# Graph attention over sorted edges: softmax batches of 24 groups in place of 32, and one joint tile with one 128-column product per 128 edges

## The chip, the cores and the metric

The kernel runs on one core of one Trainium2 chip. The metric is the time that the device takes for one execution, in microseconds (us). The kernel before takes 5138.95 us, the median of 3 runs (5133.07 to 5140.92).

A core has engines that run side by side, each through its own list of instructions: TensorE (PE in the profile; PEld are its weight loads), VectorE (DVE), ScalarE (ACT), GpSimd (POOL) and SyncE (SP). They wait for each other by semaphores. Transfers between DRAM and on-chip memory are DMAs: an engine issues them, and they run apart from it.

## The reference: what is computed

One layer of a graph network with attention: 12,500 nodes with 64 features each (`x`), and 400,000 directed edges with 64 features each (`edge`), sorted by their destination `dst`.

```python
h_src, h_dst = nfeats[src], nfeats[dst]
e = leaky_relu(concat([h_src, h_dst, efeats]) @ W_attn + b_attn, 0.01)[:, 0]
m = concat([h_src, efeats]) @ W_ne
ex = exp(e - segment_max(e, dst)[dst])
alpha = ex / segment_sum(ex, dst)[dst]
z = segment_sum(alpha[:, None] * m, dst)
out = layernorm(x + relu(concat([nfeats, z]) @ W_out))
```

Each edge gets a score, the scores are normalised by a softmax over the edges of one destination, and the edges' messages are summed with these weights. `W_ne` is linear, so the kernel sums the raw features (the source's row and the edge's features) with the weights alpha, and multiplies by `W_ne` and `W_out` once per node at the end.

## The kernel before

**Tiling.** The edges are cut into 782 groups of 512 (128 partitions x 4 edges). Four groups make a part, and up to 32 groups (`BG`) a softmax batch. The list `sizes` (L345 to L353) is [30], 23 times 32, then 12 and 4: 26 batches, 196 parts; a full batch has 8 parts.

**A part, up to its scores.** `gather` (L134 to L153) takes two tiles: `ze` for the edge features and `zx` for the rows of the sources. SyncE issues one DMA for the part's edge features (L140): 512 KB, where each partition gets 1024 adjacent bytes per group. GpSimd issues 16 indirect DMAs (L149), each of which fetches 128 rows, one per partition. In later batches the row comes from a DRAM table, whose rows hold the 64 features and, in column 64, the source's part of the score. The first batch ("plain") starts before that table is there: it fetches from `x` itself and works out the score in L169 to L171. `scores` (L155 to L185) is VectorE's: multiply the edge features by their weights (L165), reduce (L167), add the source's score (L172), build `hot`, a 0/1 matrix that says which of 48 neighbouring nodes (`S`) an edge goes to (L174), add the destination's score (L179 to L183; it comes as a row `wrow` by a SyncE DMA, L159, and is spread over the partitions by TensorE, L161), leaky ReLU (L184). The scores go into the batch's tile `y`.

**A batch.** When all parts of a batch are scored, `softmax` (L224 to L319) normalises the whole batch at once. It transposes `y` (L252), runs scans along the sorted destinations, with small TensorE products between them to carry values across rows (L190, L198), and leaves `alpha` (L307). It takes from the batch before the carried maximum and sum (`carry`), and it needs the destinations of the neighbouring edges, `d3`, which `neighbours` (L203) loads by four SyncE DMAs (L218). A batch smaller than `BG` clears `d3` and `y` first (L208 and in the main loop).

**A part, after its softmax.** `aggregate` (L321 to L342): VectorE makes the weights `w` = `hot` x `alpha` (L324). TensorE multiplies: for each of 4 groups and 4 edges per partition, one product with `ze` as its weights and one with `zx` (L332), 64 columns each, written to the lower and the upper 64 partitions of `pg`; `w` with its 48 columns moves through. That is 32 products per part; each appears in the trace as two weight loads and two matmuls (float32). VectorE then adds `pg` to `acc`, which holds the sums of all nodes on chip (L342).

```python
pg = psum.tile([P, SG, P], F32, name="pg")[:, :, 0:S]
for g in range(n):
    for t in range(T):
        for at, z in ((0, ze), (D, zx)):
            nc.tensor.matmul(pg[at:at + D, g, :], z[:, g, t, 0:D], w[:, g, t, :],
                             start=(t == 0), stop=(t == T - 1))
```

**Buffers.** `ze` and `zx` have 11 buffers each (`ZB`), so that 11 parts can be on chip between their gathers and their products; `hot` has 9 (`HB`), `w` and `pg` have 2, `d3` and `y` 2, `alpha` 1. A gather into a tile has to wait until the products of the part that had the tile are over.

**What sets the order.** All loops are unrolled when the program is built. The framework puts each engine's instructions in order by a planner with estimated costs, and adds the semaphores; on the chip each engine keeps its order. SyncE's list has the edge features, `wrow`, `d3` and the index loads; GpSimd's has the indirect gathers and little else; ScalarE's has copies, exponentials and DMAs for other work. Five parts of the first batch are gathered ahead of the main loop (L369, L415).

**Around the loop.** In the first 300 us or so the kernel also prepares the table. In batches from the third on, `own_part` (L432; L446, L450) does one piece of x @ W_out after each part's sums, until all nodes are done. `finish_sorted` (L491) multiplies `acc` by the joint weights (L538), adds, normalises and stores.

Of the kernel before, what the change touches and what calls it, by code (L numbers as in the profile page):

```python
# [9 lines left out]
F32 = mybir.dt.float32  # L10
I32 = mybir.dt.int32
AF = mybir.ActivationFunctionType
OP = mybir.AluOpType
AX = mybir.AxisListType

P = 128
T = 4
GE = P * T
# [7 lines left out]
S = 48  # L26
BG = 32
SG = 4
HQ = 4
EW = 65  # L30
ZB = 11
HB = 9
NBC = 4
# [5 lines left out]
def sorted_path(ctx, tc, x, dst, idx, edge, w_ne, w_attn, b_attn, w_out, out, flag):  # L39
# [6 lines left out]
    nc = tc.nc  # L46
    N, D = x.shape
# [6 lines left out]
    RP = REST // T  # L54
# [36 lines left out]
    feats = loop.enter_context(tc.tile_pool(name="feats", bufs=ZB))  # L91
# [41 lines left out]

    def gather(g0, n, srcs, b0, plain):  # L134

        ze = feats.tile([P, SG, T, D], F32, name="ze")
        zx = feats.tile([P, SG, T, EW], F32, name="zx")
        whole = min(n, NG - 1 - g0)
        if whole:
            nc.sync.dma_start(out=ze[:, 0:whole].rearrange("p g t f -> p g (t f)"),  # L140
                              in_=edge[g0 * GE:(g0 + whole) * GE, :].rearrange("(g p t) f -> p g (t f)", g=whole, t=T))
        if whole < n:
            nc.vector.memset(ze[:, n - 1], 0.0)
            nc.sync.dma_start(out=ze[0:RP, n - 1],
                              in_=edge[E - REST:E, :].rearrange("(p t) f -> p t f", t=T))
        for g in range(n):
            for t in range(T):
                at = srcs[:, t, g0 + g - b0:g0 + g - b0 + 1]
                nc.gpsimd.indirect_dma_start(  # L149
                    out=zx[:, g, t, 0:D] if plain else zx[:, g, t, :], out_offset=None,  # L150
                    in_=x[:, :] if plain else table[:, :],
                    in_offset=bass.IndirectOffsetOnAxis(ap=at, axis=0))
        return ze, zx  # L153

    def scores(g0, n, ze, zx, drel, b0, y, plain):  # L155

        b = g0 - b0
        wrow = tiny.tile([1, SG, S], F32, name="wrow")
# [3 lines left out]

        yb = y[:, :, b:b + n].rearrange("p t g -> p g t")
        prod = work.tile([P, SG, T, D], F32, name="prod", bufs=1)
        nc.vector.tensor_tensor(prod[:, 0:n], ze[:, 0:n],  # L165
                                w_edge.unsqueeze(1).to_broadcast([P, n, T, D]), op=OP.mult)
        nc.vector.tensor_reduce(yb, prod[:, 0:n], axis=AX.X, op=OP.add)  # L167
        if plain:
            nc.vector.tensor_tensor(prod[:, 0:n], zx[:, 0:n, :, 0:D],  # L169
                                    w_src.unsqueeze(1).to_broadcast([P, n, T, D]), op=OP.mult)  # L170
            nc.vector.tensor_reduce(zx[:, 0:n, :, D], prod[:, 0:n], axis=AX.X, op=OP.add)  # L171
        nc.vector.tensor_tensor(yb, yb, zx[:, 0:n, :, D], op=OP.add)  # L172
        hot = work.tile([P, SG, T, S], BF16, name="hot", bufs=HB)
        nc.vector.tensor_tensor(  # L174
            hot[:, 0:n], slots.unsqueeze(1).unsqueeze(1).to_broadcast([P, n, T, S]),
# [1 line left out]
            op=OP.is_equal)  # L177
# [140 lines left out]
            nc.vector.tensor_copy(fac, pfac[:, 0:1])  # L318
        return alpha, fac, (top[:, R:R + 1], den[:, R:R + 1])  # L319

    def aggregate(g0, n, ze, zx, hot, alpha, b0, fac):  # L321
        b = g0 - b0
        w = work.tile([P, SG, T, S], F32, name="w")
        nc.vector.tensor_tensor(  # L324
            w[:, 0:n], hot[:, 0:n],
            alpha[:, :, b:b + n].rearrange("p t g -> p g t").unsqueeze(3).to_broadcast([P, n, T, S]),
            op=OP.mult)
        pg = psum.tile([P, SG, P], F32, name="pg")[:, :, 0:S]
        for g in range(n):
            for t in range(T):  # L330
                for at, z in ((0, ze), (D, zx)):
                    nc.tensor.matmul(pg[at:at + D, g, :], z[:, g, t, 0:D], w[:, g, t, :],  # L332
                                     start=(t == 0), stop=(t == T - 1))
        _, vs = nc.values_load_multi_w_load_instructions(
            d0i[0:1, g0:g0 + n], engines=(EngineType.DVE,), min_val=0, max_val=N - 1,
            skip_runtime_bounds_check_because=within)
        for g in range(n):
            if g == 0 and fac is not None:
                a1 = acc[:, ds(vs[0], 1)]
                nc.vector.tensor_scalar(a1, a1, fac, None, op0=OP.mult)  # L340
            ag = acc[:, ds(vs[g], S)]
            nc.vector.tensor_tensor(ag, ag, pg[:, g, :], op=OP.add)  # L342
# [1 line left out]

    sizes = []  # L345
    left = NG
    for short in (SG, 3 * SG):
        sizes.insert(0, short)
        left -= short
    while left > 0:  # L350
        sizes.insert(0, min(left, BG))
        left -= sizes[0]
    starts = [sum(sizes[:k]) for k in range(len(sizes))]  # L353

# [105 lines left out]
    with loop:  # L460
# [3 lines left out]
        for k, G in enumerate(sizes):  # L464
# [6 lines left out]
            parts = []  # L471
            for g0 in range(b0, b0 + G, SG):
                n = min(SG, b0 + G - g0)
                ze, zx = ahead.pop(0) if ahead else gather(g0, n, srcs, b0, k == 0)
                hot = scores(g0, n, ze, zx, drel, b0, y, k == 0)
                parts.append((g0, n, ze, zx, hot))
            if k + 2 < len(sizes):
                ready[k + 2] = prepare(k + 2)
            alpha, fac, carry = softmax(G, y, d3, carry, k == 0)
            for g0, n, ze, zx, hot in parts:  # L480
                aggregate(g0, n, ze, zx, hot, alpha, b0, fac if g0 == b0 else None)
                if own < NB and k > 1:
                    own_part(own)
                    own += NBC
# [521 lines left out]
```

## Time and profile before

| what | value |
|---|---|
| median of 3 runs | 5138.95 us |
| the profiled execution: its time | 5109.14 us |
| its span, first to last instruction | 5107.4 us |
| mean granted TensorE clock, share of full speed | 0.547 |
| one stretch from alpha to alpha (2113 to 2315 us): span | 202.00 us |
| in it: PE, PEld busy | 51.86 and 41.17 us |
| in it: DVE, ACT, POOL busy | 64.57, 2.73 and 120.84 us |
| in it: DMA engines busy, moved | 0.19, 43 GB/s |
| indirect gathers of 128 rows (L149) | 3008 from the table, 120 from `x` |
| softmax batches, parts | 26, 196 |

How to read the lines further down. The page's first section gives each engine's busy time, its share of the span and its number of instructions. A row of a group names the line, the engine, the operation and the tiles (out<-in), then after the bar its busy time and the mean duration in ns, then the idle time of the engine just ahead of these instructions and what ended most of it; "issue" is time in which the engine waited for nothing that the profile shows. A row of the waits names the engine and the tile it then wrote, what it waited for, and the sum in us, the number of waits, and the longest. A row in order of time gives start and duration in us, and in square brackets the idle time before it. The 40 slices of the page say how busy an engine is over time:

```profile
PE   0022233443222222222222222222222222222226
DVE  3333233232342332332323323323233233233346
POOL 6645656556556556565565565655655655656550
PEclk9975555555555555555555555555555555555555
```

Each digit is a busy share in tenths for 127.7 us (a fortieth of the span), or, in the last row, the clock that TensorE was granted. The main loop looks alike from one end to the other.

### The profile page before, as it was taken

How to read it: one execution, taken by the hardware profiler on the slowest of the kernel's cores; microseconds unless marked ns; L12 is line 12 of the kernel's file. 1: busy time of each engine (PE TensorE's matmuls, PEld its weight loads, DVE VectorE, ACT ScalarE, POOL GpSimd, SP SyncE). 2: the span in 40 equal slices, each digit the busy share in tenths (PEclk: the TensorE clock that was granted, in tenths of full speed). 3: DMA queues.
4: the chain of work that ended last, by engine and by line, in shares of the span. 5: the costliest groups of instructions: out<-in, count | busy, mean ns of one | idle time of the engine just before them, and what ended most of it. 6: DMA issues, size and time to landing. Idle time of an engine off the chain costs nothing.

```text
span 5107.4 us, 39846 instructions
## 1 busy us (share of the span) xinstructions
PE 1410.6 (28%) x14238; PEld 1105.0 (22%) x14238; DVE 1708.1 (33%) x4006; ACT 109.6 (2%) x239; POOL 2964.9 (58%) x3142
## 2 busy tenths in 40 slices
PE   0022233443222222222222222222222222222226
PEld 0012122332222122212121212122222211221225
DVE  3333233232342332332323323323233233233346
ACT  0000000000000000000000000000000000000001
POOL 6645656556556556565565565655655655656550
PEclk9975555555555555555555555555555555555555
DMA  6111122222111112111111111111111211212113
GB/s 145 25 34 42 44 48 54 53 53 60 41 45 44 43 38 48 42 46 41 43 44 43 42 44 43 43 42 44 47 41 40 47 42 38 47 37 48 41 36 77
DMA packets 315273, 239.73 MB, mean 47 GB/s; under 512 B 160576, under 2 KB 264235, under 8 KB 315064
## 3 DMA queue, kind: packets, MB, share of 16 engines
q0 software_dynamic: 100320, 104.41, 10.6%
q1 hardware_dynamic: 147464, 116.22, 8.0%
q10 hardware_dynamic: 67280, 16.45, 1.6%
q8 instruction: 115, 1.88, 0.2%
q14 instruction: 94, 0.77, 0.1%
HBM read 226.98 MB, written 12.28 MB: 47 GB/s over the span
## 4 chain that ended last, share of the span: by engine, by line
issue 28%; POOL 26%; another core or an unknown queue 19%; DVE 14%; PE 10%; DMA 3%; DVEq 1%; ACT 0%; POOLq 0%; ACTq 0%
POOL zx L149 26%; PE pg L332 7%; DMA zx<-table,srcs 2%; DVE y L167 2%; DVE prod L165 2%; DVE sdst L182 1%; DVE prod L179 1%; PE sm L198 1%; PE sm L190 1%; DVE hot L174 1%; DVE w L324 1%; DVE by_row L195 0%; DVE b L271 0%; DVE acc L342 0%
## 5 line engine op out<-in xcount | busy, mean ns | idle before, releaser
L149 POOL DMA_INDIRECT zx<-table,srcs x3008 | 2840.6, 944 | 1951.4 <-issue 841.3
L332 PE MATMUL pg<-w,ze 128*64 128x48 f32 x6256 | 792.3, 297 | 1640.2 <-issue 985.1
L332 PEld LDWEIGHTS pg<-w,ze 128*64 128x64 f32 x6256 | 703.6, 213 | 1729.3 <-issue 1581.7
L332 PE MATMUL pg<-w,zx 128*64 128x48 f32 x6256 | 803.4, 297 | 613.2 <-issue 582.1
L324 DVE TENSOR_TENSOR w<-hot,alpha 128x768 f32<-128x768 bf16 x196 | 184.0, 949 | 2208.2 <-remote 1135.9
L332 PEld LDWEIGHTS pg<-w,zx 128*64 128x64 f32 x6256 | 706.7, 213 | 656.3 <-issue 621.7
L342 DVE TENSOR_TENSOR acc<-acc,pg 128x48 f32 x782 | 153.9, 197 | 812.7 <-remote 742.1
L161 PE MATMUL win<-wrow,ones_row 1*128 1x192 f32 (+1 forms) x392 | 182.0, 552 | 746.8 <-DVE prod L179 433.1
L161 PEld LDWEIGHTS win<-wrow,ones_row 1*128 1x128 f32 x392 | 92.9, 284 | 810.4 <-DVE prod L179 448.3
L165 DVE TENSOR_TENSOR prod<-ze,fixed 128x1024 f32<-128x1024 f32 x196 | 236.9, 1209 | 19.9 <-issue 19.9
L167 DVE TENSOR_REDUCE y<-prod 128x16 f32<-128x1024 f32 x196 | 236.1, 1205 | 2.4 <-DVE y L184 2.3
L182 DVE TENSOR_REDUCE sdst<-prod 128x16 f32<-128x768 f32 x196 | 185.1, 944 | 4.3 <-DVE prod L179 2.4
L179 DVE TENSOR_TENSOR prod<-hot,win 128x768 f32<-128x768 bf16 x196 | 185.4, 946 | 0.9 <-issue 0.2
L174 DVE TENSOR_TENSOR hot<-fixed,drel 128x768 bf16<-128x768 f32 x196 | 185.6, 947 | 0.0
L149 POOL DMA_INDIRECT zx<-in_x_dram,srcs x120 | 116.9, 974 | 51.5 <-issue 36.3
L112 ACT ACTIVATE nat<-raw 32x1024 f32<-32x1024 int32 (+3 forms) x26 | 27.5, 1056 | 3242.2 <-PE pp L115 1762.9
L450 PE MATMUL pg<-wout,xtt 64*128 64x64 f32 x196 | 47.4, 418 | 132.0 <-ACT xtt L447 132.0
L198 PE MATMUL sm<-ones_row,by_row 1*128 1x1 f32 x208 | 59.2, 351 | 81.2 <-DVE by_row L195 66.2
L198 PEld LDWEIGHTS sm<-ones_row,by_row 1*128 1x128 f32 x208 | 50.9, 302 | 131.5 <-DVE by_row L195 104.2
L190 PE MATMUL sm<-order,b 128*1 128x128 f32 x104 | 30.1, 391 | 163.8 <-DVE b L271 158.4
L450 PEld LDWEIGHTS pg<-wout,xtt 64*128 64x128 f32 x196 | 42.8, 319 | 148.3 <-ACT xtt L447 148.3
L190 PE MATMUL sm<-order,s 128*1 128x128 f32 x104 | 30.3, 393 | 147.7 <-issue 57.1
(133 smaller groups left out, 949.1 us busy)
## 6 DMA issues: line engine op xcount, KB each, us to landing
ze<-in_edge_dram SPq DMA_DIRECT2D x194, 512.0 KB
zx<-table,srcs POOLq DMA_INDIRECT x3008
table<-xt ACTq DMA_DIRECT2D x14, 227.5 KB
wrow<-wins SPq DMA_DIRECT2D x195, 0.8 KB
xb<-in_x_dram ACTq DMA_DIRECT2D x24, 128.0 KB
early<-xo ACTq DMA_DIRECT2D x24, 128.0 KB
xb<-in_x_dram ACTq DMA_DIRECT2D x12, 256.0 KB
xo<-early SPq DMA_DIRECT2D x12, 256.0 KB
```

The costliest lines, as they stand in the source:

```text
L149: nc.gpsimd.indirect_dma_start(out=zx[:, g, t, 0:D] if plain else zx[:, g, t, :], out_offset=None, in_=x[:, :] if plain else table[:, :], ...
L161: nc.tensor.matmul(win[:, 0:n, :], ones_row, wrow[:, 0:n, :], start=True, stop=True)
L165: nc.vector.tensor_tensor(prod[:, 0:n], ze[:, 0:n], w_edge.unsqueeze(1).to_broadcast([P, n, T, D]), op=OP.mult)
L167: nc.vector.tensor_reduce(yb, prod[:, 0:n], axis=AX.X, op=OP.add)
L174: nc.vector.tensor_tensor(hot[:, 0:n], slots.unsqueeze(1).unsqueeze(1).to_broadcast([P, n, T, S]), drel[:, :, b:b + n].rearrange("p t g -> ...
L179: nc.vector.tensor_tensor(at[:, 0:n], hot[:, 0:n], win[:, 0:n].unsqueeze(2).to_broadcast([P, n, T, S]), op=OP.mult)
L182: nc.vector.tensor_reduce(sdst[:, 0:n], at[:, 0:n], axis=AX.X, op=OP.add)
L190: nc.tensor.matmul(p[0:1, :], col, order, start=True, stop=True)
L198: nc.tensor.matmul(p[:, 0:1], by_row, ones_row[:, 0:1], start=True, stop=True)
L324: nc.vector.tensor_tensor(w[:, 0:n], hot[:, 0:n], alpha[:, :, b:b + n].rearrange("p t g -> p g t").unsqueeze(3).to_broadcast([P, n, T, S]) ...
L332: nc.tensor.matmul(pg[at:at + D, g, :], z[:, g, t, 0:D], w[:, g, t, :], start=(t == 0), stop=(t == T - 1))
L342: nc.vector.tensor_tensor(ag, ag, pg[:, g, :], op=OP.add)
```

## The change

The constant `BS` = 24 sets the size of a full batch; the tiles keep their size for 32 (`BG`). With the last two batches of 10 and 4, `sizes` is 32 times 24, then 10 and 4: 34 batches, 196 parts, 6 parts in a full batch. Since every batch is now smaller than `BG`, each clears its `d3` and `y`.

The two tiles of a part become one, `z`, with 129 columns per edge: edge features in 0 to 63, the gathered row in 64 to 128. It keeps 11 buffers. SyncE now issues one DMA per group for the edge features (four per part), in pieces of 256 bytes, since an edge's features no longer lie beside the next one's on chip. One product with 128 weight columns takes the place of two with 64. The number and shape of the gathers, and VectorE's work per part, stay.

```diff
@@ -26,8 +26,10 @@
 S = 48
 BG = 32
 SG = 4
+BS = 24
 HQ = 4
 EW = 65
+ZW = 129
 ZB = 11
 HB = 9
 NBC = 4
@@ -133,26 +135,25 @@
 
     def gather(g0, n, srcs, b0, plain):
 
-        ze = feats.tile([P, SG, T, D], F32, name="ze")
-        zx = feats.tile([P, SG, T, EW], F32, name="zx")
+        z = feats.tile([P, SG, T, ZW], F32, name="z")
         whole = min(n, NG - 1 - g0)
-        if whole:
-            nc.sync.dma_start(out=ze[:, 0:whole].rearrange("p g t f -> p g (t f)"),
-                              in_=edge[g0 * GE:(g0 + whole) * GE, :].rearrange("(g p t) f -> p g (t f)", g=whole, t=T))
+        for g in range(whole):
+            nc.sync.dma_start(out=z[:, g, :, 0:D],
+                              in_=edge[(g0 + g) * GE:(g0 + g + 1) * GE, :].rearrange("(p t) f -> p t f", t=T))
         if whole < n:
-            nc.vector.memset(ze[:, n - 1], 0.0)
-            nc.sync.dma_start(out=ze[0:RP, n - 1],
+            nc.vector.memset(z[:, n - 1, :, 0:D], 0.0)
+            nc.sync.dma_start(out=z[0:RP, n - 1, :, 0:D],
                               in_=edge[E - REST:E, :].rearrange("(p t) f -> p t f", t=T))
         for g in range(n):
             for t in range(T):
                 at = srcs[:, t, g0 + g - b0:g0 + g - b0 + 1]
                 nc.gpsimd.indirect_dma_start(
-                    out=zx[:, g, t, 0:D] if plain else zx[:, g, t, :], out_offset=None,
+                    out=z[:, g, t, D:2 * D] if plain else z[:, g, t, D:ZW], out_offset=None,
                     in_=x[:, :] if plain else table[:, :],
                     in_offset=bass.IndirectOffsetOnAxis(ap=at, axis=0))
-        return ze, zx
-
-    def scores(g0, n, ze, zx, drel, b0, y, plain):
+        return z
+
+    def scores(g0, n, z, drel, b0, y, plain):
 
         b = g0 - b0
         wrow = tiny.tile([1, SG, S], F32, name="wrow")
@@ -162,14 +163,14 @@
 
         yb = y[:, :, b:b + n].rearrange("p t g -> p g t")
         prod = work.tile([P, SG, T, D], F32, name="prod", bufs=1)
-        nc.vector.tensor_tensor(prod[:, 0:n], ze[:, 0:n],
+        nc.vector.tensor_tensor(prod[:, 0:n], z[:, 0:n, :, 0:D],
                                 w_edge.unsqueeze(1).to_broadcast([P, n, T, D]), op=OP.mult)
         nc.vector.tensor_reduce(yb, prod[:, 0:n], axis=AX.X, op=OP.add)
         if plain:
-            nc.vector.tensor_tensor(prod[:, 0:n], zx[:, 0:n, :, 0:D],
+            nc.vector.tensor_tensor(prod[:, 0:n], z[:, 0:n, :, D:2 * D],
                                     w_src.unsqueeze(1).to_broadcast([P, n, T, D]), op=OP.mult)
-            nc.vector.tensor_reduce(zx[:, 0:n, :, D], prod[:, 0:n], axis=AX.X, op=OP.add)
-        nc.vector.tensor_tensor(yb, yb, zx[:, 0:n, :, D], op=OP.add)
+            nc.vector.tensor_reduce(z[:, 0:n, :, 2 * D], prod[:, 0:n], axis=AX.X, op=OP.add)
+        nc.vector.tensor_tensor(yb, yb, z[:, 0:n, :, 2 * D], op=OP.add)
         hot = work.tile([P, SG, T, S], BF16, name="hot", bufs=HB)
         nc.vector.tensor_tensor(
             hot[:, 0:n], slots.unsqueeze(1).unsqueeze(1).to_broadcast([P, n, T, S]),
@@ -318,7 +319,7 @@
             nc.vector.tensor_copy(fac, pfac[:, 0:1])
         return alpha, fac, (top[:, R:R + 1], den[:, R:R + 1])
 
-    def aggregate(g0, n, ze, zx, hot, alpha, b0, fac):
+    def aggregate(g0, n, z, hot, alpha, b0, fac):
         b = g0 - b0
         w = work.tile([P, SG, T, S], F32, name="w")
         nc.vector.tensor_tensor(
@@ -328,9 +329,8 @@
         pg = psum.tile([P, SG, P], F32, name="pg")[:, :, 0:S]
         for g in range(n):
             for t in range(T):
-                for at, z in ((0, ze), (D, zx)):
-                    nc.tensor.matmul(pg[at:at + D, g, :], z[:, g, t, 0:D], w[:, g, t, :],
-                                     start=(t == 0), stop=(t == T - 1))
+                nc.tensor.matmul(pg[:, g, :], z[:, g, t, 0:2 * D], w[:, g, t, :],
+                                 start=(t == 0), stop=(t == T - 1))
         _, vs = nc.values_load_multi_w_load_instructions(
             d0i[0:1, g0:g0 + n], engines=(EngineType.DVE,), min_val=0, max_val=N - 1,
             skip_runtime_bounds_check_because=within)
@@ -344,11 +344,11 @@
 
     sizes = []
     left = NG
-    for short in (SG, 3 * SG):
+    for short in (SG, 10):
         sizes.insert(0, short)
         left -= short
     while left > 0:
-        sizes.insert(0, min(left, BG))
+        sizes.insert(0, min(left, BS))
         left -= sizes[0]
     starts = [sum(sizes[:k]) for k in range(len(sizes))]
 
@@ -471,14 +471,14 @@
             parts = []
             for g0 in range(b0, b0 + G, SG):
                 n = min(SG, b0 + G - g0)
-                ze, zx = ahead.pop(0) if ahead else gather(g0, n, srcs, b0, k == 0)
-                hot = scores(g0, n, ze, zx, drel, b0, y, k == 0)
-                parts.append((g0, n, ze, zx, hot))
+                z = ahead.pop(0) if ahead else gather(g0, n, srcs, b0, k == 0)
+                hot = scores(g0, n, z, drel, b0, y, k == 0)
+                parts.append((g0, n, z, hot))
             if k + 2 < len(sizes):
                 ready[k + 2] = prepare(k + 2)
             alpha, fac, carry = softmax(G, y, d3, carry, k == 0)
-            for g0, n, ze, zx, hot in parts:
-                aggregate(g0, n, ze, zx, hot, alpha, b0, fac if g0 == b0 else None)
+            for g0, n, z, hot in parts:
+                aggregate(g0, n, z, hot, alpha, b0, fac if g0 == b0 else None)
                 if own < NB and k > 1:
                     own_part(own)
                     own += NBC
```

## The prediction

> **What bounds the kernel now.** I read the page first, then the list of waits, then GpSimd's (POOL), VectorE's (DVE) and TensorE's (PE) instructions in order of time over one batch (2113 to 2315 us), and last the same distances in every other batch.
>
> ```profile
> span 5107.4 us, 39846 instructions
> PE 1410.6 (28%) x14238; PEld 1105.0 (22%) x14238; DVE 1708.1 (33%) x4006; ACT 109.6 (2%) x239; POOL 2964.9 (58%) x3142
> issue 28%; POOL 26%; another core or an unknown queue 19%; DVE 14%; PE 10%; DMA 3%; DVEq 1%; ACT 0%; POOLq 0%; ACTq 0%
> L149 POOL DMA_INDIRECT zx<-table,srcs x3008 | 2840.6, 944 | 1951.4 <-issue 841.3
> L332 PE MATMUL pg<-w,ze 128*64 128x48 f32 x6256 | 792.3, 297 | 1640.2 <-issue 985.1
> ```
>
> No engine is full. POOL is the fullest, and its real cost is more than 944 ns: its gathers start every 1.248 us (0.30 us of issue between them). 3008 of them make 3754 us; the 120 of the first batch run from 17 to 175 us. So 3912 us of the 5107 are gathers in sequence, and about 1200 us are something else. The waits tell what:
>
> ```profile
> PEld pg L332 <- issue: 2203.4, 1099, 20.3
> DVE w L324 <- remote: 1135.9, 74, 20.9
> POOL zx L149 <- PE pg L332: 786.6, 62, 61.1
> ```
>
> POOL waits for products (L332) that free a gather tile. Within one batch:
>
> ```profile
> 2096.80 0.94 POOL L149 DMA_INDIRECT zx<-table,srcs  x1 [0.30 <-issue]
> 2118.71 0.94 POOL L149 DMA_INDIRECT zx<-table,srcs  x1 [20.97 <-PE pg L332]
> ...
> 2157.39 0.94 POOL L149 DMA_INDIRECT zx<-table,srcs  x1 [0.30 <-issue]
> 2165.31 0.94 POOL L149 DMA_INDIRECT zx<-table,srcs  x1 [6.97 <-PE pg L332]
> ```
>
> The first wait (21 us) comes once per batch: eight tiles hold the batch, three hold the next one's first parts, and the twelfth needs the batch's first product, which needs its softmax. The others are 3.1 us per part, or 6.5 per two parts. One batch is therefore 128 x 1.248 = 160 us of gathers and 42 us of waits: 202 us, and 24 batches keep to that within a few us.
>
> Why are the products late? When POOL stands still, a part's 64 matmuls take 3.7 us. While it gathers, they crawl:
>
> ```profile
> 2136.71 0.31 PE L332 MATMUL pg<-w,ze 128*64 128x48 f32 x1
> 2139.19 0.24 PE L332 MATMUL pg<-w,zx 128*64 128x48 f32 x1 [2.17 <-issue]
> 2141.99 0.24 PE L332 MATMUL pg<-w,ze 128*64 128x48 f32 x1 [2.56 <-issue]
> ...
> 2163.69 0.24 PE L332 MATMUL pg<-w,zx 128*64 128x48 f32 x1 [0.46 <-issue]
> ```
>
> With weight loads counted, one instruction starts per 0.7 or 1.4 us, until about 5 us after POOL has stopped; then the rest goes at once. Even matmuls that have started are reported late:
>
> ```profile
> 2119.46 0.20 DVE L342 TENSOR_TENSOR acc<-acc,pg 128x48 f32 x1
> 2132.92 0.95 DVE L324 TENSOR_TENSOR w<-hot,alpha 128x768 f32<-128x768 bf16 x1 [13.26 <-remote]
> ```
>
> This w needed a buffer whose last matmul the trace shows over at 2121.8; DVE was let on at 2132.9. No row names the cause. What the trace does show is a count: of a part's 128 PE instructions (weight loads and matmuls), 61 to 64 start at once when the part begins in the middle of a POOL run, about 95 to 101 when it begins 2.9 us after POOL's restart, and all 128 when POOL stands. So POOL and PE hold each other: PE recovers when POOL stops, and POOL stops because PE is late.
>
> **The change part by part.** *Gathers:* the same 3128 at 1.248 us: nothing.
>
> *One product per 128 edges.* Matmuls and weight loads at L332 fall from 25,024 to 12,512, 64 per part. Each gets longer. The nearest row has 128 weight columns:
>
> ```profile
> 5039.63 17.33 PE L538 MATMUL po<-both,acc 128*128 128x64 f32 x80 [0.32 <-DVE both L520]
> ```
>
> That is 0.217 us per matmul with its load, 64 columns moving; a pair of today's 64-column halves goes in 0.105 us. With 48 columns moving I take 0.19 to 0.21, so 32 matmuls take 6.0 to 6.8 us with POOL standing, against 3.7: **plus 2.3 to 3.1 us** wherever a product is what POOL waits for. The page "TensorEngine Tiling (Array Packing)" of the Trainium skill, section "Theoretical Speedup", says the same against this change: two tiles of at most 64 columns work up to twice as fast. By that rule alone this part of the change would be a loss, at most 196 x 3.1 = 610 us. Against it stands the count above: 64 instructions are what a part gets through before it crawls. The pauses that products cause now (3.1 us per part) can thus lie between 0 and 3.1 + 3.1 = 6.2 us. I take **1.5 us**, half of today's for half the instructions: 196 x 1.5 = 294 us.
>
> *Batches of 24 with eleven tiles.* Six tiles hold the batch and five lie ahead: 80 gathers, 100 us, instead of 60. From the eighth product's end to the next alpha today are 35 us (2280 to 2315), and alpha to the first product 5: 40 us fit in 100 if the products keep up with POOL; then the wait of 21 us goes. If they lag until all eleven tiles are in use, it stays. Bounds 0 to 21 per batch; I take **8**, nearer the lower end because tile slack grows. There are 34 batches in place of 26, some 33 with the wait: 264 us. The eight further softmaxes (22.7 us each from transposing y to alpha, 18.9 in the first batch) are otherwise beside POOL; without that cover they cost 8 x 22.7 = 182 us, which is part of the slower rival.
>
> *Start and end.* The first batch has 6 parts in place of 7.5; a plain part costs DVE some 8 us, so its alpha moves from 294 to about 282, while eleven tiles are full at about 246: the wait there falls from 61 to about 40. The tail after the last gather (4970.6 to 5107.4) I leave at 137.
>
> *Edits costed at nothing.* Edge features in four DMAs per part: SyncE issues 4 x 0.39 = 1.6 us per part against 20 us of gathers. Their pieces shrink from 1024 to 256 bytes: q1's packets take 46 ns in the median, its 256-byte ones 18, so 100,000 x 46 becomes 400,000 x 18 ns, 288 to 450 us on each of 16 engines: hidden. Uncovered, a part would wait at most some 2 us more for its landing, 400 us in all. "DMA: Bandwidth & Descriptors" of the Trainium skill, section "Specifications", asks for at least 512 bytes per piece; the row (4 x 18 = 72 against 46 ns) shows a loss of 1.6 times, on engines that are 20% busy. The memsets of d3 and y (167 and about 140 ns, 32 batches more) are 10 us of DVE, which is 33% busy. The wait they add is SyncE's: d3's loads follow the memset, and wrow and edge loads queue behind them. Today d3 is loaded two batches early (2113.5, right after its buffer is read), so nobody is at that door; if the memset slid behind a batch's sums, edge loads could not run ahead, and that would add to the slower rival. DVE reads with a stride of 129 as it does with 65 (L169, 1.22 us, against L165's 1.21): nothing.
>
> **The sum**, on the profiled execution (span 5107.4, run 5109.1, 30 us under the median 5138.95): 17 to the first gather + 3912 + 40 + 137 = 4106; + 294 + 264 = 4664. Plus 2 around the span and 30 to the median: **4696; I say 4690.** The same form gives today's: 17 + 3912 + 61 + 137 = 4127, and 24 x 41 = 980 us of waits make 5107.
>
> **The rivals.**
>
> *POOL alone.* 64 instructions fit, products stay ahead, and waits vanish: 4106 + 32 = 4138, up to 4300 with a few pauses. For it: the burst of 61 to 64 and the slack of five tiles. Against: the longer product, and no row in which POOL runs for a whole batch beside products.
>
> *Slower: the products keep POOL's pace and the softmax comes more often.* If a part's products are released only when POOL stops, whatever their number, six parts take what six take today: from alpha at 2113.0 to the sixth part's release at 2233.9, 121 us. Then 35 us to the next alpha: 156 us per 24 groups, against 151.5 for the same 24 today. From 282: 31 x 156 + 162 from the last full batch's alpha to the end (as today from 4945) = 5280, + 32 = 5312. With six products longer by 2.7 us, 172 per batch: 5800. It decides from 151.5 us per batch. For it: completions are late even when started, and they came at POOL's stop in most parts. Against: half the instructions, and the sixth part's tile no longer ties the softmax to late gathers.
>
> *No effect:* the pace per group stays at 6.31 us by chance. Little speaks for it.
>
> **How the numbers follow.** Forecast case (4300 to 5000): 0.34. POOL alone (4138 to 4300): 0.20. Gains under that (5000 to 5128): 0.04. Within 0.2%, about what a measurement of this kernel can tell from no change: 0.02. Slower: 0.40, two thirds of it under 5450. So faster 0.58, same 0.02, slower 0.40. Range: 4150 to 5450 leaves out about 0.02 below and 0.14 above. The faster cases alone span 4140 to 5000.
>
> **What would show it.** Right: POOL's idle time per batch of 96 gathers is 10 to 20 us; the wait before the part whose tile the first product frees is under 10 us; PE's issue wait at the product falls to well under half of 2203 us; a part's 64 PE instructions start within 8 us. POOL alone: 120 us from alpha to alpha. Slower: over 151.5 us from alpha to alpha, POOL idle about 35 us of it, with 20 again before each batch's first freed tile. Wrong outright: if gathers wait for edge loads in the joint tile, if SyncE stands at d3, or if L149's rhythm leaves 1.25 us.

## The result, and the profile after

The changed kernel takes 5374.86 us (median of 4 runs, 5371.27 to 5382.75) against 5137.34 us (4 runs): a ratio of 1.0465, 95% interval 1.0447 to 1.0483. It is slower; the forecast was 4690 us. The profiled execution took 5372.95 us.

From the page of the changed kernel (now L150 is the gather, L325 makes w, L332 is the joint product):

```profile
span 5371.2 us, 30757 instructions
PE 1945.6 (36%) x8238; PEld 1723.2 (32%) x8238; DVE 1750.1 (33%) x4448; ACT 131.1 (2%) x287; POOL 2973.2 (55%) x3142
L150 POOL DMA_INDIRECT z<-table,srcs x3032 | 2872.1, 947 | 2171.5 <-PE pg L332 1039.1
L332 PE MATMUL pg<-w,z 128*128 128x48 f32 x6256 | 1387.0, 405 | 1653.6 <-issue 743.5
```

Its waits:

```profile
DVE w L325 <- remote: 1284.4, 58, 36.6
POOL z L150 <- PE pg L332: 1039.1, 60, 56.4
PEld pg L332 <- issue: 775.8, 403, 9.4
```

PE waits far less inside a part's products (776 us where it was 2203), as the forecast had it, but POOL waits more for them (1039 us, was 787). The wait did not go; it moved. ("remote" is a wait whose releaser the profile could not name.) POOL's stops in one batch of the changed kernel (start, duration, and in brackets the idle time before it; the gathers without a stop are left out):

```profile
2850.92 0.94 POOL L150 DMA_INDIRECT z<-table,srcs  x1 [27.40 <-PE pg L332]
...
2896.89 0.94 POOL L150 DMA_INDIRECT z<-table,srcs  x1 [6.27 <-remote]
...
2942.96 0.95 POOL L150 DMA_INDIRECT z<-table,srcs  x1 [6.38 <-PE pg L332]
...
3010.53 0.94 POOL L150 DMA_INDIRECT z<-table,srcs  x1 [27.86 <-PE pg L332]
```

Two stops of 6 us, and one of 28 us ahead of the sixth part, whose tile the batch's first product frees: that is the softmax's place. From alpha to alpha are 160 us, over the 151.5 that decide.

The first stop of 6 us shows what POOL stands for. The last product of the part whose tile it needs, on PE, and the next thing that waits for the same semaphore, on VectorE:

```profile
2875.84 0.24 PE L332 MATMUL pg<-w,z 128*128 128x48 f32 x1 [1.89 <-issue]
```

```profile
2896.65 0.95 DVE L325 TENSOR_TENSOR w<-hot,alpha 128x768 f32<-128x768 bf16 x1 [34.83 <-remote]
```

The product is over at 2876.1 by the profile, and the part's last increment of the semaphore, for which VectorE and POOL both wait, comes at 2896.6, when POOL has stood for 6 us. In 27 batches such a delay is 18 to 32 us.

The sum of the prediction, term by term, with what the two traces hold (POOL's idle times of over 0.5 us, each less the 0.3 us of issue that every gather has, added up by their place; each column adds up to its span):

| term, us | before | forecast | after |
|---|---|---|---|
| to the first gather | 16.7 | 17 | 14.8 |
| 3128 gathers with their issue | 3909.8 | 3912 | 3918.6 |
| stops of the first batches | 69.6 | 40 | 65.5 |
| stops for products inside a batch | 496.5 | 294 | 406.7 |
| stops for the first product after a softmax | 478.0 | 264 | 784.3 |
| last gather to the end | 136.8 | 137 | 181.4 |
| span | 5107.4 | 4664 | 5371.2 |

The softmax's stop is 520 us off; all else together is 187.

### The profile page after: what moved, and what is told of

It reads as the page before. It is cut to its first block, busy times and chain, and to the rows that moved or that the text cites. A ratio compares the mean times of both kernels' runs of the same rounds, so it can differ in the third digit from the quotient of the medians.

```text
span 5371.2 us, 30757 instructions
## 1 busy us (share of the span) xinstructions
PE 1945.6 (36%) x8238; PEld 1723.2 (32%) x8238; DVE 1750.1 (33%) x4448; ACT 131.1 (2%) x287; POOL 2973.2 (55%) x3142
## 4 chain that ended last, share of the span: by engine, by line
another core or an unknown queue 27%; issue 25%; DVE 15%; PE 15%; POOL 13%; DMA 3%; DVEq 1%; ACTq 0%; ACT 0%; POOLq 0%; SPq 0%
PE pg L332 13%; POOL z L150 13%; DVE prod L166 2%; DMA z<-table,srcs 2%; DVE hot L175 2%; DVE prod L180 1%; DVE sdst L183 1%; DVE y L168 1%; PE win L162 1%; DVE w L325 1%; PE sm L191 1%; DVE by_row L196 0%; DVE b_s L303 0%; DVE acc L342 0%
## 5 line engine op out<-in xcount | busy, mean ns | idle before, releaser
L150 POOL DMA_INDIRECT z<-table,srcs x3032 | 2872.1, 947 | 2171.5 <-PE pg L332 1039.1
L332 PE MATMUL pg<-w,z 128*128 128x48 f32 x6256 | 1387.0, 405 | 1653.6 <-issue 743.5
L332 PEld LDWEIGHTS pg<-w,z 128*128 128x128 f32 x6256 | 1372.3, 329 | 1719.7 <-issue 775.8
L325 DVE TENSOR_TENSOR w<-hot,alpha 128x768 f32<-128x768 bf16 x196 | 183.1, 948 | 1551.9 <-remote 1284.4
L162 PE MATMUL win<-wrow,ones_row 1*128 1x192 f32 x392 | 194.3, 586 | 390.8 <-issue 223.2
L199 PE MATMUL sm<-ones_row,by_row 1*128 1x1 f32 x272 | 78.3, 354 | 675.5 <-DVE by_row L196 347.5
L199 PEld LDWEIGHTS sm<-ones_row,by_row 1*128 1x128 f32 x272 | 67.5, 306 | 739.6 <-issue 433.5
L166 DVE TENSOR_TENSOR prod<-z,fixed 128x1024 f32<-128x1024 f32 x196 | 236.4, 1206 | 54.0 <-DMA z<-table,srcs 53.6
L150 POOL DMA_INDIRECT z<-in_x_dram,srcs x96 | 93.7, 976 | 42.2 <-issue 29.0
L201 DVE COPY col<-sm 128x1 f32<-128x1 f32 x136 | 20.2, 149 | 199.8 <-remote 145.2
L248 PE MATMUL sm<-order,whole 128*1 128x128 f32 x204 | 49.6, 409 | 61.4 <-issue 36.1
```

The source lines that it names most:

```text
L150: nc.gpsimd.indirect_dma_start(out=z[:, g, t, D:2 * D] if plain else z[:, g, t, D:ZW], out_offset=None, in_=x[:, :] if plain else table[:, :],
L162: nc.tensor.matmul(win[:, 0:n, :], ones_row, wrow[:, 0:n, :], start=True, stop=True)
L166: nc.vector.tensor_tensor(prod[:, 0:n], z[:, 0:n, :, 0:D], w_edge.unsqueeze(1).to_broadcast([P, n, T, D]), op=OP.mult)
L199: nc.tensor.matmul(p[:, 0:1], by_row, ones_row[:, 0:1], start=True, stop=True)
L325: nc.vector.tensor_tensor(w[:, 0:n], hot[:, 0:n], alpha[:, :, b:b + n].rearrange("p t g -> p g t").unsqueeze(3).to_broadcast([P, n, T, S]) ...
L332: nc.tensor.matmul(pg[:, g, :], z[:, g, t, 0:2 * D], w[:, g, t, :], start=(t == 0), stop=(t == T - 1))
```

## The experiments

Each run is compared with the kernel before on its own chip, and here the chips differ: the kernel before takes 4105 to 4114 us on four of them (called prompt below), and 5124 and 5134 us on two others (called late), as the 5137 us of the first measurement.

### The parts of the change, one by one

e1: the kernel before, smaller batches alone.

```diff
-    for short in (SG, 3 * SG):
+    for short in (SG, 10):
...
-        sizes.insert(0, min(left, BG))
+        sizes.insert(0, min(left, BS))
```

> The kernel before with batches of 24 alone (32 x 24, 10, 4); two tiles and two products per 128 edges stay. Theory A (a chain of latencies sets the time: from alpha to alpha it is the batch's parts times a pace, plus the softmax; a part's products pace at 22.4 us with 64-column halves and 18.2 with joint products; a softmax takes 22.7 us where POOL stands and 51 where POOL gathers beside it): 6 x 22.4 + 51 = 185 us per batch, 31 x 185 + 457 for start and end = about 6200 us, far slower than the changed kernel. Rival B (the pace per part has nothing to do with the joint product; the batch size is the whole change): 160 us per batch, about 5375 us as the changed kernel. Rival C (the joint tile with its 256-byte pieces and its one semaphore increment per product is what costs): under 5137 us.

e2: the changed kernel with the old sizes.

```diff
-BS = 24
+BS = 32
-    for short in (SG, 10):
+    for short in (SG, 3 * SG):
```

> The changed kernel with the batch sizes of before (30, 23 x 32, 12, 4): joint tile and joint product alone. Theory A: eight parts and three tiles ahead, so POOL stands during the softmax: 8 x 18.2 + 22.7 = 168 us per 32 groups against 202, which makes 5137 - 24 x 34 = about 4320 us; if POOL gathers during the softmax after all, 8 x 18.2 + 51 = 197 us, about 5010. Rival B: no change, 5137 us. Rival C: slower than 5375 us, since the loss comes with the joint tile.

e3: the changed kernel with fewer tiles.

```diff
-ZB = 11
+ZB = 9
```

> The changed kernel with 9 buffers of the joint tile in place of 11, so that three tiles lie ahead of a batch of six, as three lay ahead of eight before. Theory A: POOL stands during the softmax, which falls from 51 to some 23 us; a batch is 6 x 18.2 + 23 = 132 us in place of 160, the whole about 5375 - 31 x 28 = 4510 us. Rival D (what PE gets done is bought by POOL's standing still, about 40 us per batch whichever way it is spread): 160 us per batch as with 11 buffers, about 5375. Rival E (fewer tiles are only less slack): slower than 5375.

e4: the changed kernel with two products again.

```diff
-                nc.tensor.matmul(pg[:, g, :], z[:, g, t, 0:2 * D], w[:, g, t, :],
-                                 start=(t == 0), stop=(t == T - 1))
+                for at in (0, D):
+                    nc.tensor.matmul(pg[at:at + D, g, :], z[:, g, t, at:at + D], w[:, g, t, :],
+                                     start=(t == 0), stop=(t == T - 1))
```

> The changed kernel with its joint tile, but two products of 64 columns per 128 edges again, from the two halves of the tile. Theory A: the pace per part goes back to 22.4 us: 6 x 22.4 + 51 = 185 us per batch, about 6200 us, as with batches of 24 alone. Rival B: no change against 5375. Rival C (semaphore increments or the length of the 128-column products cost): under 5375, about 5137 or less. A difference between this and the run with two tiles is what the joint tile and its four edge DMAs cost by themselves.

All four ran on one prompt chip, where the kernel before takes 4105.27 us, so the expected numbers, which are for a late chip, were not put to the test. Measured: e1 4083.90 us, ratio 0.9947 (0.9931 to 0.9964); e2 4151.27, 1.0112 (1.0095 to 1.0129); e3 4380.63, 1.0671 (1.0653 to 1.0689); e4 4084.62, 0.9951 (0.9935 to 0.9968). Two things follow all the same. e1 and e4 differ in the joint tile, in its four edge DMAs per part and in the stride: 0.7 us, so these cost nothing here; on a late chip that pair was not run. And the joint product costs time even here: e2, with the joint tile, takes 46 us more than before, and its trace has 163 us from the last gather to the end, where the kernel before has 118 (on another prompt chip, in f2). Smaller batches alone gain a little. e3 lost to its shorter slack (POOL stops 13 us in 16 of the batches, and 69 us in the first); of theory A it says nothing.

### The two kernels themselves, on another chip

f1 is the changed kernel, f2 the kernel before; f3 and f4 repeat e1 and e2.

> The changed kernel once more. The four runs before this one found the kernel before at 4105 us and no lateness: the median time from a small matmul's end to its semaphore was 0.01 us with POOL gathering, where the first measurement's trace has 2.2 us (before) and 3.4 us (changed). Theory L (on the chip of the first measurement PE's completions come late while POOL gathers, and that lateness is what the change was paid in): where the kernel before takes 4105 us, POOL alone sets the pace, 120 us per batch of 24, and the changed kernel takes 4090 to 4150 us, within 1% of before; where it takes 5137 us, the changed kernel takes about 5375 again. Rival M (the joint product is slower by itself, whatever the chip): over 2% slower than before here too.

> The kernel before, for its trace on this chip. Theory L: if it takes about 4105 us, POOL never waits over 0.6 us in the steady batches, the softmax runs beside POOL, and a small matmul's semaphore comes 0.01 us after its end in the median; if it takes about 5137 us, the picture of the first trace (21 us of standing still per batch, 2.2 us of lateness).

> Batches of 24 alone (two tiles, two products of 64 columns), once more, for the case that this chip is late with PE's completions. Theory A there: 6 parts at 22.4 us and a softmax of 51 us, 185 us per batch, about 6200 us; rival B there: 160 us per batch, 5375 us. On a chip without the lateness: 4084 us again.

> Joint tile and joint product alone with batches of 32, once more, for the same case. Theory A on a late chip: 8 x 18.2 + 22.7 = 168 us per 32 groups, about 4320 us, or 197 us and 5010 if POOL gathers during the softmax; rival B: 5137 us. On a chip without the lateness: 4151 us again.

Another prompt chip: before 4113.81 us; f1 4138.68, ratio 1.0062 (1.0045 to 1.0078); f3 4091.79, 0.9946 (0.9926 to 0.9966); f4 4158.77, 1.0109 (1.0089 to 1.0129). The kernel before on this chip, from its page and its waits:

```profile
span 4111.7 us, 39846 instructions
L149 POOL DMA_INDIRECT zx<-table,srcs x3008 | 2853.2, 949 | 961.9 <-issue 882.1
POOL zx L149 61%; DMA zx<-table,srcs 6%; PE pg L332 2%; DVE w L324 0%; DVE prod L165 0%; PE sm L198 0%; DVE sdst L182 0%; DVE y L167 0%; PE sm L190 0%; DMA d0i<-in_dst_dram 0%; PE po L538 0%; DVE prod L169 0%; DVE b_s L302 0%; DVE zx L171 0%; DVE hot L174 0%
```

```profile
POOL zx L149 <- PE pg L332: 45.4, 2, 45.1
```

The same gathers of 949 ns, and the chain of what ended last is POOL's: of 787 us of waits for products 45 are left, one wait in the first batch. The changed kernel stops there once too (31.0 us, 14 less than the 44.8 of before), and loses 40 us at the end: 157.9 us from the last gather against 118.1, since the longer products of the last batches have no gathers beside them. So on a prompt chip the forecast's rival "POOL alone" (4138 us) is what happens. That the number fits to the microsecond is luck: it has 137 us for the end, where 158 were measured, and adds 30 us for the distance of the profiled run from the median.

What differs between the chips can be read at a softmax's small products, which have nothing else in their way. First the changed kernel on the late chip, PE and then VectorE:

```profile
2962.85 0.55 PE L199 MATMUL sm<-ones_row,by_row 1*128 1x1 f32 x2 [9.68 <-issue]
```

```profile
2962.36 0.34 DVE L196 COPY by_row<-top 1x128 f32<-1x128 f32 x1
2966.70 0.16 DVE L201 COPY col<-sm 128x1 f32<-128x1 f32 x1 [4.00 <-remote]
```

And the same place on the prompt chip:

```profile
2114.10 0.55 PE L199 MATMUL sm<-ones_row,by_row 1*128 1x1 f32 x2 [1.02 <-DVE by_row L196]
```

```profile
2113.70 0.26 DVE L196 COPY by_row<-top 1x128 f32<-1x128 f32 x1
2114.70 0.16 DVE L201 COPY col<-sm 128x1 f32<-128x1 f32 x1 [0.74 <-PE sm L199]
```

The product is over 0.55 us after its start in both. VectorE may go on 0.05 us later on the prompt chip, and 3.3 us later on the late one. Over all such products with POOL gathering beside them, the time from the modelled end to the semaphore is 0.01 us in the median on the prompt chip, in either kernel, and on the late chip over 2 us (before) and over 3 us (after; one in ten some 8 or more). With POOL standing for 6 us or more it is 0.01 us there too.

### On a late chip: whose gathers, which product

g1: no indirect gathers.

```diff
-                at = srcs[:, t, g0 + g - b0:g0 + g - b0 + 1]
-                nc.gpsimd.indirect_dma_start(
+                r0 = ((g0 + g) * T + t) % NFULL * P
+                nc.sync.dma_start(
...
+                    in_=x[r0:r0 + P, :] if plain else table[r0:r0 + P, :])
```

> The kernel before, with each of GpSimd's indirect gathers replaced by a plain DMA of the same shape (128 rows of 260 bytes, here neighbouring rows of the table) that SyncE issues: the rows are not those of the sources, so the output is another one. GpSimd has nothing to do in the loop. What bounds the kernel on a chip without the lateness: if POOL's gathers alone do (theory L), this falls far below 4105 us, towards VectorE's work (some 65 us busy and 10 of waits per batch of 32, about 2200 to 2600 us); if the rows' transfers bound it, it stays above 3500. On a chip with the lateness: if the lateness comes with GpSimd's gathers, a small matmul's semaphore is 0.01 us late in the median; if with the transfers, 2 us again.

g2 is e4 once more. g3 is e1 with a first batch of 12:

```diff
-    for short in (SG, 10):
+    for short in (SG, 10, 12):
```

> The joint tile with two products of 64 columns and batches of 24, once more, in case this chip shows the lateness: there, theory A gives 6 x 22.4 + 51 = 185 us per batch, about 6200 us, and rival B 160 us, about 5375. On a chip without it 4085 to 4092 us again.

> Batches of 24 with two tiles and two products, and the first batch of 12 groups (12, 31 x 24, 12, 10, 4). On a chip without the lateness the only long wait of POOL left is that of the first batch (45 us before, some 24 with 24 groups first). Theory L: with 12 groups the first softmax comes earlier and the wait goes: 4084 - 20 = about 4065 us, a per cent under before. Rival N (batch 1 gathers from the table, which is not ready earlier): 4084 us or more.

A late chip: before 5124.00 us; g1 2230.56; g2 5095.93; g3 5059.60, ratio 0.9875 (0.9858 to 0.9891).

```profile
span 2228.8 us, 39743 instructions
PE 1043.6 (47%) x14238; PEld 853.2 (38%) x14238; DVE 1719.2 (77%) x4006; ACT 110.0 (5%) x239; POOL 7.6 (0%) x14
PEld pg L331 <- issue: 231.8, 117, 3.0
```

With g1 the lateness is gone (0.01 us in the median over all small products, 0.02 for all but one in a hundred), though the same number of rows of 260 bytes arrives in less than half the time. So it comes with GpSimd's indirect gathers, not with the bytes. The rows of g1 are neighbours, which the gathers' are not, and SyncE issues them; these differences were not tried alone.

g2 says which part of the change hurts on a late chip: batches of 24 and the joint tile together are 0.5% faster than before (one execution), and the single product is what brings 5096 to 5375 us. The two times are from different late chips, whose kernels before are 13 us apart. g2's waits, and its products where they are not late:

```profile
POOL z L150 <- PE pg L333: 565.2, 49, 53.1
```

```profile
1046.57 3.65 PE L333 MATMUL pg<-w,z 128*64 128x48 f32 x64 [3.49 <-DVE w L325]
2408.36 5.71 PE L333 MATMUL pg<-w,z 128*64 128x48 f32 x120 [4.98 <-DVE w L325]
```

A part's 64 matmuls in a run of their own take 3.65 us; the 120 of two parts, one behind the other, take 5.71. The granted clock of TensorE is 0.50 in the first stretch and 0.61 in the second. The changed kernel's 32:

```profile
2898.85 7.06 PE L332 MATMUL pg<-w,z 128*128 128x48 f32 x32 [22.76 <-DVE acc L342]
```

### Why the joint product costs there: its messages or its length

The framework posts one semaphore increment for several products only on a product that has no wait of its own. With two halves the edge products have none, and a part posts 2 increments (392 in the trace of before); each joint product waits for its gather, and a part posts up to 16 (3014 after). h1 reverses the order of a part's joint products, which leaves one increment of 16 (203 in its trace).

```diff
-        for g in range(n):
-            for t in range(T):
+        for g in reversed(range(n)):
+            for t in reversed(range(T)):
...
-                                 start=(t == 0), stop=(t == T - 1))
+                                 start=(t == T - 1), stop=(t == 0))
```

> The changed kernel with the order of a part's 16 joint products reversed. The last 8 of them then have no wait of their own, and the framework posts one semaphore increment of 16 per part in place of 16 increments of one; products, tiles and batches stay. Theory S (on a chip where PE's completions come late while GpSimd gathers, each increment that PE posts is a late message, and the joint product lost by posting 16 per part where two were posted before): where the kernel before takes about 5125 us, this falls from 5375 to 5100 or less. Rival W (the longer 128-column products lose there, whatever they post): about 5375. Where the kernel before takes 4105 us no message is late, and both say 4130 to 4140 us, as the changed kernel.

h2 is e4 with the halves in the outermost loop:

```diff
-        for g in range(n):
-            for t in range(T):
-                for at in (0, D):
+        for at in (0, D):
+            for g in range(n):
+                for t in range(T):
```

> Joint tile, batches of 24 and two products of 64 columns, but all 16 products of the edge half ahead of the 16 of the gathered half. The latter have a wait each, so PE posts 17 increments per part in place of two; the products are the short ones. Theory S on a chip with late completions: it loses what the changed kernel lost, from 5096 to about 5375 us. Rival W: about 5096. Where the kernel before takes 4105 us, both say about 4085 to 4092 us.

Late again, before 5133.94 us: h1 5348.70, ratio 1.0418 (1.0395 to 1.0441); h2 5246.02, 1.0222 (1.0205 to 1.0239). Theory S falls for the joint product: fifteen increments less are worth 26 us of 279 (the changed kernel itself ran on another late chip). h2 is 150 us over g2; it also moves the gathered half behind the edge half, so how much of that the increments cost is not shown.

i1 and i2 leave out half of the products, i1 in the changed kernel and i2 in e4; i3 is g3 again.

```diff
-            for t in range(T):
+            for t in range(T // 2):
...
-                                 start=(t == 0), stop=(t == T - 1))
+                                 start=(t == 0), stop=(t == T // 2 - 1))
```

> The changed kernel with 2 of the 4 joint products per group left out (half of the edges are missing from the sums): a part's products take some 3.5 us with POOL standing in place of 7.0, with 128 columns each as before. Theory W (on a chip with late completions, kernel before about 5130 us, the joint product loses by its length, since it is what POOL waits for): 5375 falls by some 280 us, to 5100 or less, as with the short halves (3.7 us). Rival V (the length is not it: a part is released when POOL stands, or joint products are late as such): about 5350 to 5375. Where the kernel before takes 4105 us: only the end is shorter, about 4090 to 4110.

> The joint tile with two products of 64 columns and batches of 24, with the same half of the products left out: some 1.9 us per part in place of 3.7. Theory W on a chip with late completions: (5375 - 5096) / 3.3 = 85 us per us of a part's products, so 5096 - 1.8 x 85 = about 4940 us. Rival V: about 5096. Where the kernel before takes 4105 us: about 4070 to 4090.

> Batches of 24 with a first batch of 12, two tiles and two products, which took 5060 us where the kernel before took 5124. Where the kernel before takes 4105 us: about 4065 us, since the only long wait of POOL, at the first batch, goes; on a chip with late completions 0.988 of before again.

A prompt chip, before 4105.67 us: i1 4098.65, i2 4082.63, i3 4081.14, ratio 0.9938 (0.9921 to 0.9954). In i3 the first batch's stop went, but stops of 21.0 and 9.7 us came ahead of it, between 78 and 122 us: rival N had the mechanism, and its 4084 us or more is nearer than theory L's 4065. j1 and j2 are i1 and i2 on other chips:

> The changed kernel with half of its joint products left out (half of the edges are missing from the sums), once more, for a chip with late completions (kernel before about 5130 us). Theory W: about 280 us less than 5375, 5100 or less, since a part's products take 3.5 us in place of 7.0; rival V: 5350 to 5375. Where the kernel before takes 4105 us: 4099 us again.

> The joint tile with two products of 64 columns, batches of 24, and half of the products left out (half of the edges are missing from the sums), once more. On a chip with late completions (kernel before about 5130 us) theory W, that time goes with the length of a part's products: 1.9 us in place of 3.7 at (5375 - 5117) / 3.5 = 74 us per us makes 5096 - 1.8 x 74 = about 4965 us. If the length matters only above some 3.5 us: about 5096. Where the kernel before takes 4105 us: 4083 us again.

j1 fell on a late chip (before 5133.94) and took 5117.41 us; j2 on a prompt one (before 4106.47, j2 4079.19), so how the halves scale on a late chip stays open. j1:

```profile
span 5115.4 us, 24470 instructions
POOL z L150 <- PE pg L332: 702.6, 35, 52.9
```

Half of the joint products give back 257 of the 279 us (one execution). It is the time on TensorE that goes with the loss, not the number of instructions: a part has 64 (loads and matmuls) in 7.06 us with the joint product, 32 in 3.65 us in j1, 128 in 3.65 us in g2, for 5375, 5117 and 5096 us (the kernel before beside them at 5137, 5134 and 5124). POOL's stops per batch of 96 gathers (batches 9 to 28) show where it goes, in us ahead of each of the six parts:

| | 1 | 2 | 3 | 4 | 5 | 6 (softmax) | sum |
|---|---|---|---|---|---|---|---|
| g2, halves | 3.0 | 3.4 | 3.3 | 3.4 | 3.3 | 15.4 | 31.8 |
| after, joint | 0.1 | 6.0 | 0.1 | 6.1 | 0.1 | 28.1 | 40.4 |
| h1, one increment | 0.1 | 5.7 | 0.1 | 5.8 | 0.1 | 27.7 | 39.4 |
| j1, half | 0.1 | 0.1 | 0.6 | 10.2 | 0.3 | 20.4 | 31.6 |

## Why the prediction was wrong

**The step that failed** is the softmax's: "then the wait of 21 us goes", priced at 8 us per batch between 0 and 21. It is 28 in the steady batches, outside its own bounds (12 to 20 in the seven after the first), and 784 us in all for 264. The step rested on two things, and neither held on this chip.

The first was "if the products keep up with POOL". They start soon enough: in 150 of 196 parts all 64 PE instructions start within 8 us, as the forecast asked. But they are reported late. The part at 2876 waits 20.6 us for its semaphore, until POOL has stood for 6 us, and POOL's stops ahead of each second part say that all eleven tiles were in use again, the prediction's own condition for "it stays".

The second was a softmax of 22.7 us that costs nothing beside POOL. That time was measured with POOL mostly standing: it gathered in a third of it. With five tiles ahead it gathers in two thirds, and the softmax takes 52.6 us on average (27 batches, 23.0 before). VectorE is idle for 27 of them where it was for 7, mostly for the small products' late results, and it works for 19 us on other parts, their scores above all, where that was 6. So the waits are some two thirds of the growth. In one softmax that I followed, 24 us are waits for PE; the longest:

```profile
2961.86 0.47 DVE L264 TENSOR_TENSOR_SCAN top<-rw,top,sm 1x128 f32<-1x128 f32 x1 [9.33 <-remote]
```

A long softmax is not enough to make POOL stop. On the prompt chip the changed kernel's takes 59 us with POOL gathering all the time, since VectorE has the next parts' scores in its list and waits there for their rows, and no stop follows:

```profile
2139.21 0.19 DVE L173 TENSOR_TENSOR y<-y,z 128x16 f32<-128x16 f32 x1 [13.37 <-DMA z<-table,srcs]
```

And j1's takes 53 us on a late chip, with a stop of 20 us. My reading is that it takes late products and a long softmax together; no run parted the two. On prompt chips, without lateness, the stop does go.

**The joint product's price** was mis-sized too. The forecast scaled the row of 0.217 us down to 0.19 to 0.21 because fewer columns move; it is 7.06 / 32 = 0.22, so fewer moving columns did not shorten it. The part takes 7.06 us against 3.65, plus 3.4 where 2.3 to 3.1 were forecast. Taking then half of today's pauses "for half the instructions" was the wrong measure. The stops inside a batch did shrink (496.5 to 406.7 us, forecast 294), but the longer product returns in the softmax's stop: with the halves, at the same batch size, that term is 447 us, with the joint product 784. The Trainium skill, "TensorEngine Tiling (Array Packing)", section "Theoretical Speedup", states that two tiles of at most 64 columns work up to twice as fast; the rows agree (7.06 against 3.65 us is 1.9 times), and this was the rule to heed.

**The end** (137, measured 181) was left as it was. With g2 it is 157, so some 24 us are the longer products. The other 20 came with the batches of 24 and the joint tile; on a prompt chip the same two leave the end at 114 us (118 before), and why they lengthen it on a late one is open.

**The first batch**: its long stop is 56 us (61 before, forecast 40), since its alpha comes at 295 us and not at 282. On prompt chips it falls by 14 us (44.8 to 31.0), where 21 were forecast.

**Right**: the gathers (3912, measured 3918.6); the edits at nothing, edge DMAs, strides and memsets (e4 against e1, on a prompt chip: 0.7 us). "DMA: Bandwidth & Descriptors" of the Trainium skill, section "Specifications", asks for pieces of at least 512 bytes; the 256-byte pieces cost nothing that these runs can tell, on DMA engines that the changed kernel's page shows a quarter busy. Of the signs of being right, two came (PE's issue wait, and the 64 instructions within 8 us) and two did not (POOL's idle time of 40 us per batch, and the wait of 28).

**The rival "slower"** had the size (156 us per batch and 5312 in all, measured 160 and 5375) and the point from which it decides, and its mechanism, a release when POOL stops, is what the part at 2876 shows. Its sum was another: from alpha until the next y is transposed are 107 us, under the 121 for its six parts, and the softmax is longer than its 35. That the total came so near is in part luck.

**Not seen at all**: I wrote that no row names the cause of the lateness, and took it for a property of the kernel. The same kernel has it on some chips and not on others.

**Open**: why PE's completions come late on some chips while GpSimd gathers, and not on others. No run changed that on a late chip but leaving the gathers out. My theory A (a fixed pace per part, 18.2 us joint and 22.4 with halves) fell: g2 has 18.2 with halves as well; my reading, which no run tested, is that gathers that run in the softmax's time are missing from the rest of the batch.

e1 with a first batch of 12 is a little faster than the kernel before on both kinds of chip: 0.9875 of it on a late one, 0.9938 on a prompt one, where e1 alone had 0.9947.

## What to carry to other kernels

A duration read beside a standing engine is a duration with that engine standing: before you move work under a cover, look up how it ran when the cover was at work. Where a wait of one engine is what lets another catch up, taking the wait away moves it to the next chain of round trips, here the softmax. A matmul that has started, or is over in the profile, has not yet released anybody: look at when its waiter goes on. And take the kernel before on a second chip before you explain a wait. Two products on the halves of the array can be shorter than one across it, whatever the number of instructions says.

## What the runs showed of the hardware

The same program took 4105 to 4114 us on four chips and 5124 to 5139 on others, with gathers of the same length (949 and 944 ns). Of the two traces' difference of 996 us, POOL's stops are 991 (1044.1 against 53.5 us); they go with semaphores of TensorE that come over 2 us in the median of the small products, and 7 us or more for one in ten, after the matmul's end while GpSimd issues indirect gathers.

The granted clock of TensorE is on record as 0.55 to 0.64 in every kernel with the two halves (PE 23 to 47% busy) and as 1.0 in every kernel with the joint product, but the traces of the latter hold no row of the clock, and their 1.0 does not mean a faster TensorE. The 80 products of L538 take 17.33 us in the kernel before, at a granted clock of 0.50, and in the changed kernel just as long:

```profile
5302.85 17.33 PE L538 MATMUL po<-both,acc 128*128 128x64 f32 x80 [0.32 <-DVE both L520]
```

A part's 64 halves do follow the clock: 3.65 us at 0.50 (1046 us in g2) and 2.07 us at 1.0 (4974 us). The joint product was 7.06 us wherever a part ran through.
